# Samples 1 to 3 of a modulated linear layer by Strassen's identity, with x loaded a block earlier

## The chip, the cores and the metric

The kernel runs on one core of a Trainium2 chip. A core has TensorE (PE in the profile: matmuls, and PEld for the loading of their weights), VectorE (DVE), ScalarE (ACT), GpSimd (POOL) and SyncE (SP), which run side by side, each in its own order, and wait for each other through semaphores. DMA transfers are issued from the queues of SP, ACT and POOL and are carried by 16 DMA engines. The metric is the device time of one execution in microseconds (us). Before the change it is 1159.82 us, the median of three runs (1159.18 to 1159.86).

## What is computed

x has 4 samples of 1024 tokens with 512 features, and each sample has a condition vector. All numbers are float32. The first layer is a modulated and demodulated linear layer with a residual:

```python
ys = y * scale
d = jax.lax.rsqrt(jnp.einsum('bi,io->bo', ys * ys, weight * weight) + EPS)
out = jnp.einsum('bsi,io->bso', Efou * ys[:, None, :], weight) * d[:, None, :]
...
x = x + _L0_cond_ref(x, cond_1024, L0_cond_weight)
```

So each sample b has weights of its own (the rows of the 512x512 weight matrix scaled by ys of the sample), and each output column is scaled by d. The second layer is a mixture of experts on the result: a shared expert of width 1024 (silu(x w1) * (x w3) w2) for all tokens, and for each token two out of eight experts of width 512 (gelu between two matrices), weighted by gates; the sum divided by 3 is added to x. The change concerns the first layer alone.

## The kernel before

The 4096 tokens are cut into NB = 8 blocks of TB = 512 tokens, two for each sample (BPB = 2). KC = 4 is the number of chunks of 128 features. After the linear stage come the shared expert on blocks 0 to 5 (class Shared), the routed experts (Double, Slot), and the shared expert on blocks 6 and 7 with the gathering of the routed results. No planner orders the work: the order in which the code issues instructions is the order on each engine.

The linear stage is the loop over blk. Block 0 and the preparations (the weights' squares, the norm d, called dmod) have code of their own. For block blk it goes like this:

- load_x brings x of a block from memory in four DMAs of 256 KB, one for each group of 32 partitions, into one of the three buffers of seg3. Blocks 0 to 2 come by ACT's queue (that of block 2 is issued in norm()), the others by SP's, two blocks ahead: block blk issues the load of block blk + 2.
- turn_x (L280) transposes a chunk on VectorE, so that xT[blk] has features on partitions. There are two xT buffers, and block blk turns the x of block blk + 1.
- modulate (L268) makes the weights wm of a sample on VectorE from w0 and ys, in the block before the sample's first.
- product (L450) multiplies: for each of four output chunks oc four matmuls 128x512, one for each input chunk, into a PSUM bank of their own (pl).
- residual (L352) computes pl * dmod + xT in one VectorE instruction per chunk and writes x1T[blk], the result with features on partitions. For blocks 0 to 5 that is the tile big0 to big5, for block 6 x1T6.
- turn_back (L360) transposes the result of the block before back into rows (back), and with the last chunk store_segments issues its store to x1_d on SP (L130).
- logits_by_chunk (pq, L370) and fold_logits (pr, L386) compute the router's logits of earlier blocks on TensorE; ACT copies pq out (L379).

Between the blocks SP also loads w1 (after block 1), w3 (after block 2) and w2 (after block 4), 2 MB each, into w13 and w2_sb. VectorE makes sums of w1 and w3 for the first Shared unit (weight_sums, L431 to L434) after block 5, and sums of the tokens of block 0 (token_sums, L405 to L416) after block 6. A memset of the region called zeros, half of the tile w0t (which holds w0 before), stands on POOL after block 7; zeros is later written to memory as filling (x1s_d).

The Shared units already use Strassen's identity in Winograd's form: seven products of half size in place of eight, with sums of weights and of tokens made on VectorE. Their matmuls are 128x256 (L777, L913), and they accumulate several products in one bank, the chain, which ACT copies out between two of them.

Of the kernel before, what the change touches and what calls it, by code (L numbers as in the profile page):

```python
# [45 lines left out]
def kernel(  # L46
# [33 lines left out]
    scale = 1.0 / math.sqrt(D)  # L80
    third = 1.0 / 3.0
    early = NB - TAIL
# [15 lines left out]
    def bank_a(name):  # L98
        return ps_a.tile([P, TB], FP, tag="a", name=name)
# [12 lines left out]
    base_d = dram.tile([early * TB, D], FP, name="base_d")  # L112
    x1s_d = dram.tile([ROWS, D], FP, name="x1s_d")

    def rows_to_features(eng, tile_ap, dram_2d):

        v = dram_2d.rearrange("(g k j) o -> g j k o", g=KC, k=KC, j=Q)
        for g in range(KC):
            eng.dma_start(out=tile_ap[ts(g, Q)], in_=v[g])

    def load_segments(eng, tile_ap, dram_rows):
# [36 lines left out]
    lin = lin_ctx.enter_context(tc.tile_pool(name="lin", bufs=2))  # L158

    cond_sb = late2.tile([B, D], FP, tag="partial", name="cond_sb")  # L160
    cond_p = late2.tile([B, KC, P], FP, tag="partial", name="cond_p")
# [24 lines left out]
    def load_x(eng, blk):  # L186
        new_seg(blk)
        for g in range(KC):
            load_segments_part(eng, blk, 0, TB, g)
# [67 lines left out]
        nc.gpsimd.memset(falling[:, :, e : e + 1], float(E - e))  # L257
    steps = const.tile([P, NSLOT], FP, name="steps")
    nc.gpsimd.iota(steps, pattern=[[1, NSLOT]], base=0, channel_multiplier=0, allow_small_or_imprecise_dtypes=True)
    def by_chunk(ap):  # L260

        return ap.rearrange("p (g k j) -> p k g j", g=KC, k=KC)

    def new_wm(b):
        return lin.tile([P, KC, KC, P], FP, tag="wm", name=f"wm{b}")

    def modulate(wm, b, k):
        nc.vector.tensor_scalar(  # L268
            wm[:, k].rearrange("p k (g j) -> p k g j", g=KC),
            by_chunk(w0_sb[:, k, :]),  # L270
            ysT[:, k, b : b + 1],
            None,
            ALU.mult,
        )
# [4 lines left out]
    def turn_x(blk, k, lo=0, n=TB):  # L279
        nc.vector.transpose(xTs[blk][:, k, ds(lo, n)], segs[blk][:, ds(lo // Q, n // Q), ts(k, Q)])  # L280
# [44 lines left out]
    def norm():  # L325
        pd = bank_b("pd")
        for oc in range(KC):
            nc.tensor.matmul(
                pd[:, ds(oc * B, B)], lhsT=norm_part[:, ts(oc, P)], rhs=fold[:, :B], start=True, stop=True
            )  # L330
        pt = bank_b("pt")
        for k in range(KC):
            nc.tensor.matmul(
                pt[:, : B * E],
                lhsT=ones[:, :P],
                rhs=prod[:, k].rearrange("p b e -> p (b e)"),
                start=(k == 0),
                stop=(k == KC - 1),
            )
# [16 lines left out]
    def turn_back(blk, ks):  # L356
        if blk not in backs:
            backs[blk] = late2.tile([P, TB // Q, P], FP, tag="back", name=f"back{blk}")
        for k in ks:
            nc.vector.transpose(backs[blk][:, :, ts(k, Q)], x1T[blk][:, k, :])  # L360
        if ks[-1] == KC - 1:
            store_segments(nc.sync, x1_d[ts(blk, TB)], backs[blk])
# [3 lines left out]
    def logits_by_chunk(blk):  # L366

        pq = bank_b(f"pq{blk}")
        for k in range(KC):
            nc.tensor.matmul(  # L370
                pq[ts(k, Q)],
                lhsT=rw_pad[:, k, :],
                rhs=x1T[blk][:, k, :],
                start=True,
                stop=True,
                tile_position=(0, k * Q),
            )
        partial[blk] = late2.tile([P, TB], FP, tag="partial", name=f"partial{blk}")
        nc.scalar.activation(partial[blk], pq, AF.Copy)  # L379
# [3 lines left out]
    def fold_logits(blk, s):  # L383
        if s == 0:
            prs[blk] = bank_b(f"pr{blk}")
        nc.tensor.matmul(prs[blk][:, ds(s * E, E)], lhsT=partial[blk][:, ts(s, P)], rhs=fold, start=True, stop=True)  # L386
# [38 lines left out]
    def weight_sums(u, matrices=(0, 1)):  # L425
        for i in matrices:
# [6 lines left out]
            nc.vector.tensor_tensor(a21, a11, a21, ALU.subtract)  # L433
            nc.vector.tensor_tensor(s4, a12, s2, ALU.subtract)  # L434

    backs = {}
    for blk in range(NB):
        b = blk // BPB
        if blk < early:
            x1T[blk] = big[blk]  # L440
        elif blk == early:
            x1T[blk] = x1T6
        else:
            x1T[blk] = lin0.tile([P, KC, TB], FP, tag="w0sq", name=f"x1T{blk}")
        pas = [bank_a(f"pl{blk}_{oc}") for oc in range(KC)]
        if 2 < blk + 2 < NB:
            load_x(nc.sync, blk + 2)

        def product(oc, k, lo=0, n=TB):
            nc.tensor.matmul(  # L450
                pas[oc][:, ds(lo, n)],
                lhsT=wms[b][:, k, oc, :],
                rhs=xTs[blk][:, k, ds(lo, n)],
                start=(k == 0),
                stop=(k == KC - 1),
            )
# [18 lines left out]
        for oc in range(KC):  # L475
            if blk > 0:
                for k in range(KC):
                    product(oc, k)
                if blk > 1:
                    fold_logits(blk - 2, oc)  # L480
            if blk + 1 < NB:
                if blk > 0:
                    turn_x(blk + 1, oc)
                if (blk + 1) % BPB == 0:
                    modulate(wms[b + 1], b + 1, oc)
# [5 lines left out]
            if blk == NB - 1:  # L491
                turn_back(blk, [oc])
        if blk == 1:
            rows_to_features(nc.sync, w13[0], w1)
        if blk == 2:
            rows_to_features(nc.sync, w13[1], w3)
        if blk == 4:
            nc.sync.dma_start(out=w2_sb, in_=w2.rearrange("(k p) d -> p k d", p=P))
        if blk == early - 1:
            weight_sums(0)  # L500
        if blk == early:
            token_sums(0)
        if blk == NB - 1:
            weight_sums(1)
            nc.gpsimd.memset(zeros, 0.0)
# [239 lines left out]
    class Shared:  # L745
# [801 lines left out]
```

## Time and profile before

| | us |
|---|---|
| median of three runs | 1159.82 |
| the profiled execution's own time | 1163.28 |
| span of its trace, first to last instruction | 1161.5 |
| TensorE busy | 1145.1 (99%) |
| VectorE busy | 715.8 (62%) |
| ScalarE busy | 219.1 (19%) |
| GpSimd busy | 181.3 (16%) |
| mean granted clock of TensorE | 0.997 |

The page gives the busy time of each engine, then "the chain of work that ended last": followed back from the last instruction, at each step to what released it. The timeline shows the instructions of an engine in order of time: start, duration, engine, line, operation, what it writes and reads, the shape, how many such follow each other, and in brackets the idle time before it and what ended it. Durations of neighbouring instructions overlap a little; the step from one start to the next is what an instruction costs its engine. A float32 matmul stands as two passes in the trace, so four matmuls are "x8". The windows view gives, for each stretch, the busy time of each engine with its number of instructions, the granted clock of TensorE, the busy share of the DMA engines and the GB/s that they moved.

The linear stage takes the first 137.3 us of the span (the first matmul of a Shared unit, ch, starts there). From 27 us on TensorE is busy in it without a break.

### The profile page before, as it was taken

What the parts mean: (1) busy time and instruction counts of PE and PEld (TensorE: products, weight loads), DVE (VectorE), ACT (ScalarE), POOL (GpSimd) and SP (SyncE); (2) the same over time, 40 slices, a digit from 0 to 9 for tenths busy, and PEclk for the clock granted to TensorE, in tenths of its full rate; (3) what the DMA queues carried; (4) which work ended last, traced back from release to release, by engine and by line L of the source; (5) the groups of instructions that cost most, each with busy time, mean ns of one, the idle gap of its engine ahead of it and who ended that gap; (6) DMA issues with size and microseconds to landing.
All of it is one profiled execution on the core that took longest, in us unless ns stands there. A gap on an engine that the chain in (4) does not pass through costs nothing.

```text
span 1161.5 us, 14179 instructions
## 1 busy us (share of the span) xinstructions
PE 1145.1 (99%) x5078; PEld 947.2 (82%) x5078; DVE 715.8 (62%) x1484; ACT 219.1 (19%) x395; POOL 181.3 (16%) x220
## 2 busy tenths in 40 slices
PE   9999999999999999999999999999999998999998
PEld 6444588888888888888888888888888886888886
DVE  4547677945545455454677766677645553379987
ACT  2000032111111111111122222222222121121111
POOL 2000000012212122120000000000201100076850
PEclk9999999999999999999999999999999998999999
DMA  9599399323333247443255766657689883198971
GB/s 172 110 236 208 86 341 382 124 83 127 127 127 112 97 154 236 146 142 112 65 135 150 211 185 163 163 148 215 183 211 235 236 239 96 58 257 289 322 257 72
DMA packets 139373, 203.64 MB, mean 175 GB/s; under 512 B 9876, under 2 KB 67348, under 8 KB 139288
## 3 DMA queue, kind: packets, MB, share of 16 engines
q1 hardware_dynamic: 113080, 142.77, 43.8%
q0 software_dynamic: 14784, 47.24, 12.8%
q10 hardware_dynamic: 11424, 12.59, 3.7%
q8 instruction: 43, 0.70, 0.3%
q14 instruction: 42, 0.34, 0.1%
HBM read 120.76 MB, written 81.79 MB: 174 GB/s over the span
## 4 chain that ended last, share of the span: by engine, by line
PE 91%; DVE 3%; DMA 3%; issue 1%; ACT 1%; ACTq 0%; SPq 0%; DVEq 0%; POOLq 0%; POOL 0%
PE ch L777 18%; PE s L913 15%; PE d L1177 12%; PE pl L450 9%; PE se L777 8%; PE chd L1073 7%; PE ph L1222 6%; PE tw L777 4%; PE sed L1073 3%; PE yc L1280 3%; PE yo L1280 2%; PE twd L1073 2%; DMA seg<-in_x_dram 1%; PE pq L370 1%; PE f L939 1%
## 5 line engine op out<-in xcount | busy, mean ns | idle before, releaser
L929 DVE SCALAR_TENSOR_TENSOR base<-s,base 128x512 f32<-128x512 f32 x131 | 88.7, 687 | 77.5 <-PE s L913 77.4
L913 PE MATMUL s<-w_sb,hgh 128*128 128x256 f32 x496 | 122.7, 380 | 1.9 <-DVE base L929 1.9
L715 POOL DMA_INDIRECT x1s_d<-big,addr x64 | 64.9, 1015 | 349.7 <-DVE addr L714 328.7
L450 PE MATMUL pl<-xT,wm 128*128 128x512 f32 (+1 forms) x288 | 116.8, 554 | 0.5 <-DVE big L352 0.3
L822 ACT ACTIVATE hgh<-ch 128x512 f32<-128x512 f32 x96 | 57.3, 597 | 273.8 <-PE ch L777 266.0
L913 PEld LDWEIGHTS s<-w_sb,hgh 128*128 128x128 f32 x496 | 93.8, 190 | 16.2 <-DVE base L929 3.5
L450 PEld LDWEIGHTS pl<-xT,wm 128*128 128x128 f32 x288 | 52.5, 190 | 51.6 <-issue 47.6
L826 DVE TENSOR_TENSOR hgh<-se,hgh 128x512 f32<-128x512 f32 x64 | 44.1, 689 | 71.3 <-ACT hgh L822 62.3
L1349 POOL DMA_INDIRECT big<-ys_d,addr x64 | 71.1, 1111 | 106.8 <-DVE addr L1348 88.9
L125 POOL DMA_DIRECT2D xsegs<-x1s_d x40 | 23.3, 590 | 388.2 <-DVE big L994 296.4
L913 PE MATMUL s<-more,hgh 128*128 128x256 f32 x316 | 81.3, 380 | 0.9 <-DVE xsegs L929 0.9
L1194 DVE TENSOR_TENSOR yd<-d,yd 128x512 f32<-128x512 f32 x36 | 24.8, 689 | 71.1 <-ACT yd L1190 38.7
L913 PEld LDWEIGHTS s<-more,hgh 128*128 128x128 f32 x316 | 59.9, 190 | 9.7 <-DVE xsegs L929 1.3
L1177 PE MATMUL d<-big,hgh 128*128 128x256 f32 x288 | 66.1, 379 | 0.0
L777 PE MATMUL ch<-w0t,seg 128*128 128x256 f32 x256 | 61.0, 381 | 1.0 <-ACT hgh L822 1.0
L1177 PEld LDWEIGHTS d<-big,hgh 128*128 128x128 f32 x288 | 54.7, 190 | 7.4
L777 PE MATMUL ch<-t,seg 128*128 128x256 f32 x256 | 60.5, 379 | 0.0
L777 PEld LDWEIGHTS ch<-w0t,seg 128*128 128x128 f32 x256 | 48.2, 190 | 9.0 <-ACT hgh L822 2.6
L777 PEld LDWEIGHTS ch<-t,seg 128*128 128x128 f32 x256 | 48.6, 190 | 6.6
L777 PE MATMUL se<-big,w_sb 128*128 128x256 f32 x224 | 53.0, 379 | 0.0
L777 PE MATMUL ch<-big,w_sb 128*128 128x256 f32 x224 | 53.0, 379 | 0.0
L777 PE MATMUL tw<-big,w_sb 128*128 128x256 f32 x224 | 52.9, 379 | 0.0
(264 smaller groups left out, 1989.6 us busy)
## 6 DMA issues: line engine op xcount, KB each, us to landing
big<-in_L_cond_W1e_dram SPq DMA_DIRECT2D x88, 256.0 KB, 5.8
big<-in_L_cond_W2e_dram SPq DMA_DIRECT2D x22, 1024.0 KB, 5.5
x1s_d<-w0t SPq DMA_DIRECT2D x13, 1536.0 KB, 16.3
xsegs<-x1s_d SPq DMA_DIRECT2D x96, 128.0 KB, 3.1
ys_d<-yd SPq DMA_DIRECT2D x24, 512.0 KB, 4.4
x_d<-back SPq DMA_DIRECT2D x32, 256.0 KB, 4.6
big<-x_d SPq DMA_DIRECT2D x16, 512.0 KB, 3.7
base<-x_d SPq DMA_DIRECT2D x12, 512.0 KB, 5.2
```

Source lines behind the costliest of these rows:

```text
L450: nc.tensor.matmul(pas[oc][:, ds(lo, n)], lhsT=wms[b][:, k, oc, :], rhs=xTs[blk][:, k, ds(lo, n)], start=(k == 0), stop=(k == KC - 1),)
L715: ins = nc.gpsimd.indirect_dma_start(out=x1s_d, out_offset=bass.IndirectOffsetOnAxis(ap=at.bitcast(U32), axis=0), in_=staged(t // 2)[:, t ...
L777: nc.tensor.matmul(out, lhsT=lhs[:, k, :], rhs=rhs[:, k, :], start=start and k == 0, stop=k == KH - 1, skip_group_check=not start,)
L822: nc.scalar.activation(self.both[:, :, m, cols], self.chain, AF.Copy)
L826: nc.vector.tensor_tensor(r, bank, r, ALU.add)
L913: nc.tensor.matmul(out[:, s], lhsT=a[:, ts(s, P)], rhs=b, start=start and s == 0, stop=True, skip_group_check=not (start and s == 0),)
L929: nc.vector.scalar_tensor_tensor(r, bank, third, r, ALU.mult, ALU.add)
L1073: nc.tensor.matmul(bank[:, q], lhsT=lhs[:, k, q, :], rhs=rhs[:, k, :], start=start and q == 0 and k == 0, stop=k == KH - 1, skip_group_che ...
L1177: nc.tensor.matmul(out[:, i], lhsT=a[:, q, ts(i, P)], rhs=b[:, q, :], start=start and i == 0 and q == 0, stop=q == 1, skip_group_check=not ...
L1222: nc.tensor.matmul(self.ph[:, i], lhsT=weights[j][0][:, k, ts(c, P)], rhs=xg[j][:, k, :], start=(k == 0), stop=(k == KC - 1),)
L1280: nc.tensor.matmul(out, lhsT=a[:, k, :], rhs=b[:, k, :], start=start and k == 0, stop=k == HC // 2 - 1, skip_group_check=not start,)
L1349: nc.gpsimd.indirect_dma_start(out=picks[t][i], out_offset=None, in_=ys_d, in_offset=bass.IndirectOffsetOnAxis(ap=at.bitcast(U32), axis=0) ...
```

## The change

For samples 1 to 3 (blocks 2 to 7) the sixteen matmuls 128x512 of a block become seven products of half size, each of four matmuls 128x256. Block 0 and 1 stay as they were, apart from what they prepare for sample 1.

- modulate_whole makes wm on ACT and then adds 1/dmod ("undo") to the diagonal, with one VectorE instruction 128x128 per chunk (ident times undo plus wm). So the product times dmod holds the residual x already, and residual is not called for these blocks.
- sum_weights makes four sums of a sample's weights (128x512 each, on VectorE) in the block before the sample's first; sum_tokens makes four sums of a block's xT (two pieces of 256 tokens each) in the block before it.
- linear_by_halves issues the seven products into three banks (chain, two, other). ACT copies the chain out four times with dmod as scale (evict, two instructions 128x256 each), VectorE adds the other banks (add, six instructions 128x256 in a block), and the rest of a block's work stands between the products.
- The loads of x come a block earlier: block 1 issues those of blocks 3 and 4, block blk from 2 on that of block blk + 3. w1 is loaded by halves after blocks 2 and 3, w3 after block 4, w2 by halves after blocks 5 and 6.

The buffers of the sums are new ones (t_lin), parts of x1T6 and of zeros, and for the last sample a free weight buffer. The core of the diff:

```diff
+    nc.gpsimd.memset(ident, 0.0)
+    nc.gpsimd.affine_select(out=ident, in_=ident, ...)
...
         nc.vector.tensor_tensor(dmod, dmod, newt, ALU.mult)
+        nc.vector.reciprocal(undo, dmod)
...
+    def modulate_whole(b, k):
+        wm = wms[b]
+        nc.scalar.activation(
+            wm[:, k].rearrange("p k (g j) -> p k g j", g=KC),
+            by_chunk(w0_sb[:, k, :]), AF.Copy, scale=ysT[:, k, b : b + 1],
+        )
+        nc.vector.scalar_tensor_tensor(
+            wm[:, k, k, :], ident, undo[:, ds(k * B + b, 1)], wm[:, k, k, :], ALU.mult, ALU.add
+        )
...
+    def sum_weights(b, names):
+            1: (s1, a21, a22, ALU.add),
+            2: (s2, s1, a11, ALU.subtract),
+            7: (a21, a11, a21, ALU.subtract),
+            4: (s4, a12, s2, ALU.subtract),
...
+    def sum_tokens(blk, names):
+            3: (x_[:, K1, HI], x_[:, K2, HI], x_[:, K1, HI], ALU.subtract),
+            2: (t2, x_[:, K1, HI], x_[:, K1, LO], ALU.add),
+            1: (t1, x_[:, K2, HI], t2, ALU.subtract),
+            4: (t4, x_[:, K2, LO], t2, ALU.subtract),
...
+    def linear_by_halves(blk):
+        of = {1: (a11, x_[:, K1, LO]), 2: (a12, x_[:, K2, LO]), 3: (s4, x_[:, K2, HI]), 4: (a22, t4),
+              5: (s1, t1), 6: (s2, t2), 7: (a21, x_[:, K1, HI])}
...
+        product(chain, 1, True)
+        if more_w:
+            modulate_whole(b + 1, 0)
+            modulate_whole(b + 1, 1)
+        product(two, 2, True)
+        evict(0, LO)
+        turn_back(blk - 1, [0, 1])
+        if more_x:
+            turn_x(blk + 1, 0)
+        product(chain, 6, False)
+        add(two, 0, LO)
+        fold_logits(blk - 2, 0)
+        product(other, 7, True)
+        evict(1, LO)
+        if more_w:
+            modulate_whole(b + 1, 2)
+            modulate_whole(b + 1, 3)
+        if more_x:
+            for k in range(1, KC):
+                turn_x(blk + 1, k)
+        product(chain, 5, False)
+        evict(1, HI)
+        add(other, 1, HI)
+        logits_by_chunk(blk - 1)
+        for s in range(1, NS):
+            fold_logits(blk - 2, s)
+        turn_back(blk - 1, [2, 3])
+        if more_x:
+            sum_tokens(blk + 1, (3, 2, 1))
+        product(chain, 3, False)
+        evict(0, HI)
...
+        product(other, 4, False)
+        add(other, 1, LO)
+        if more_w:
+            sum_weights(b + 1, (1, 2))
+        if more_x:
+            sum_tokens(blk + 1, (4,))
+        if more_w:
+            sum_weights(b + 1, (7, 4))
...
-        if 2 < blk + 2 < NB:
-            load_x(nc.sync, blk + 2)
+        for n in (3, 4) if blk == 1 else (blk + 3,):
+            if 1 <= blk < NB - 3:
+                load_x(nc.sync, n)
...
+        if blk >= BPB:
+            linear_by_halves(blk)
+        for oc in range(KC) if blk < BPB else ():
...
+                turn_x(blk + 1, oc)
+                modulate_whole(b + 1, oc)
             residual(blk, oc, pas[oc])
...
+        if blk == BPB - 1:
+            sum_tokens(blk + 1, (3, 2))
+            sum_weights(b + 1, (1, 2))
+            sum_tokens(blk + 1, (1,))
+            sum_weights(b + 1, (7, 4))
+            sum_tokens(blk + 1, (4,))
-        if blk == 1:
-            rows_to_features(nc.sync, w13[0], w1)
-        if blk == 2:
+        if blk in (2, 3):
+            rows_to_features(nc.sync, w13[0], w1, (2 * blk - 4, 2 * blk - 3))
+        if blk == 4:
             rows_to_features(nc.sync, w13[1], w3)
-        if blk == 4:
-            nc.sync.dma_start(out=w2_sb, in_=w2.rearrange("(k p) d -> p k d", p=P))
+        if blk in (5, 6):
+            half = ts(blk - 5, HSC // 2)
+            nc.sync.dma_start(out=w2_sb[:, half], in_=w2.rearrange("(k p) d -> p k d", p=P)[:, half])
```

More of the change, by code (lines that the diff above doesn't have):

```diff
@@ L113, with rows_to_features @@
     x1s_d = dram.tile([ROWS, D], FP, name="x1s_d")
-    def rows_to_features(eng, tile_ap, dram_2d):
+    def rows_to_features(eng, tile_ap, dram_2d, groups=range(KC)):
         v = dram_2d.rearrange("(g k j) o -> g j k o", g=KC, k=KC, j=Q)
-        for g in range(KC):
+        for g in groups:
             eng.dma_start(out=tile_ap[ts(g, Q)], in_=v[g])
@@ L158 @@
     lin = lin_ctx.enter_context(tc.tile_pool(name="lin", bufs=2))
+    lin2 = lin_ctx.enter_context(tc.tile_pool(name="lin2", bufs=1))
+    ident = lin2.tile([P, P], FP, name="ident")
+    undo = lin2.tile([P, KC * B], FP, name="undo")
+    t_lin = lin2.tile([P, 2, TB], FP, name="t_lin")
     cond_sb = late2.tile([B, D], FP, tag="partial", name="cond_sb")
@@ L259 @@
     nc.gpsimd.iota(steps, pattern=[[1, NSLOT]], base=0, channel_multiplier=0, allow_small_or_imprecise_dtypes=True)
+    nc.gpsimd.memset(ident, 0.0)
+    nc.gpsimd.affine_select(
+        out=ident, in_=ident, compare_op=ALU.not_equal, fill=1.0, base=0, pattern=[[-1, P]], channel_multiplier=1
+    )
     def by_chunk(ap):
@@ L434, in weight_sums @@
             nc.vector.tensor_tensor(s4, a12, s2, ALU.subtract)
+    def modulate_whole(b, k):
+        wm = wms[b]
+        nc.scalar.activation(
+            wm[:, k].rearrange("p k (g j) -> p k g j", g=KC),
+            by_chunk(w0_sb[:, k, :]),
+            AF.Copy,
+            scale=ysT[:, k, b : b + 1],
+        )
+        nc.vector.scalar_tensor_tensor(
+            wm[:, k, k, :], ident, undo[:, ds(k * B + b, 1)], wm[:, k, k, :], ALU.mult, ALU.add
+        )
+    K1, K2 = slice(0, KH), slice(KH, KC)
@@ new lines, with halves_of, sums_of @@
+    spots = {}
+    def halves_of(b):
+        return [wms[b][:, ks, ds(2 * m, 2), :] for m in range(2) for ks in (K1, K2)]
+    def sums_of(b):
+        if b not in spots:
+            if b < B - 1:
+                at = [x1T6[:, n, :] for n in range(1, 4)]
+            else:
+                free = new_wm(B)
+                at = [free[:, n].rearrange("p k c -> p (k c)") for n in range(3)]
+            spots[b] = [v.rearrange("p (k q c) -> p k q c", k=KH, q=2) for v in at]
+        return spots[b]
@@ new lines, in sum_weights, with t_sums @@
+    def sum_weights(b, names):
+        a11, a12, a21, a22 = halves_of(b)
+        s1, s2, s4 = sums_of(b)
+        for n, (o, i0, i1, op) in {
+            1: (s1, a21, a22, ALU.add),
+            2: (s2, s1, a11, ALU.subtract),
+            7: (a21, a11, a21, ALU.subtract),
+            4: (s4, a12, s2, ALU.subtract),
+        }.items():
+            if n in names:
+                nc.vector.tensor_tensor(o, i0, i1, op)
+    def t_sums(blk):
+        last = x1T6[:, 0, :] if blk < early else zeros
+        return [v.rearrange("p (k t) -> p k t", k=KH) for v in (t_lin[:, 0], t_lin[:, 1], last)]
@@ new lines, in sum_tokens, with product, evict, add @@
+    def sum_tokens(blk, names):
+        x_ = xTs[blk]
+        t1, t2, t4 = t_sums(blk)
+        for n, (o, i0, i1, op) in {
+            3: (x_[:, K1, HI], x_[:, K2, HI], x_[:, K1, HI], ALU.subtract),
+            2: (t2, x_[:, K1, HI], x_[:, K1, LO], ALU.add),
+            1: (t1, x_[:, K2, HI], t2, ALU.subtract),
+            4: (t4, x_[:, K2, LO], t2, ALU.subtract),
+        }.items():
+            if n in names:
+                nc.vector.tensor_tensor(o, i0, i1, op)
+    def linear_by_halves(blk):
+        b = blk // BPB
+        x_ = xTs[blk]
+        a11, a12, a21, a22 = halves_of(b)
+        s1, s2, s4 = sums_of(b)
+        t1, t2, t4 = t_sums(blk)
+        chain, two, other = (bank_a(f"{n}l{blk}").rearrange("p (q t) -> p q t", q=2) for n in ("ch", "tw", "ot"))
+        of = {
+            1: (a11, x_[:, K1, LO]),
+            2: (a12, x_[:, K2, LO]),
+            3: (s4, x_[:, K2, HI]),
+            4: (a22, t4),
+            5: (s1, t1),
+            6: (s2, t2),
+            7: (a21, x_[:, K1, HI]),
+        }
+        def product(bank, n, start):
+            lhs, rhs = of[n]
+            for q in range(2):
+                for k in range(KH):
+                    nc.tensor.matmul(
+                        bank[:, q],
+                        lhsT=lhs[:, k, q, :],
+                        rhs=rhs[:, k, :],
+                        start=start and q == 0 and k == 0,
+                        stop=k == KH - 1,
+                        skip_group_check=not (start and q == 0),
+                    )
+        def evict(m, cols):
+            for q in range(2):
+                oc = 2 * m + q
+                nc.scalar.activation(
+                    x1T[blk][:, oc, cols], chain[:, q], AF.Copy, scale=dmod[:, ds(oc * B + b, 1)]
+                )
+        def add(bank, m, cols):
+            for q in range(2):
+                oc = 2 * m + q
+                r = x1T[blk][:, oc, cols]
+                nc.vector.scalar_tensor_tensor(r, bank[:, q], dmod[:, ds(oc * B + b, 1)], r, ALU.mult, ALU.add)
+        more_x = blk + 1 < NB
+        more_w = (blk + 1) % BPB == 0 and more_x
+        product(chain, 1, True)
[29 more added lines that the diff above has]
+        evict(0, HI)
+        if not more_x:
+            turn_back(blk, [0, 1])
+        product(other, 4, False)
[6 more added lines that the diff above has]
+            sum_weights(b + 1, (7, 4))
+        if not more_x:
+            turn_back(blk, [2, 3])
@@ L444 @@
             x1T[blk] = lin0.tile([P, KC, TB], FP, tag="w0sq", name=f"x1T{blk}")
-        pas = [bank_a(f"pl{blk}_{oc}") for oc in range(KC)]
-        if 2 < blk + 2 < NB:
-            load_x(nc.sync, blk + 2)
+        if blk < BPB:
+            pas = [bank_a(f"pl{blk}_{oc}") for oc in range(KC)]
+        for n in (3, 4) if blk == 1 else (blk + 3,):
+            if 1 <= blk < NB - 3:
+                load_x(nc.sync, n)
         def product(oc, k, lo=0, n=TB):
@@ L474 @@
             wms[b + 1] = new_wm(b + 1)
-        for oc in range(KC):
+        if blk >= BPB:
+            linear_by_halves(blk)
+        for oc in range(KC) if blk < BPB else ():
             if blk > 0:
@@ L478 @@
                     product(oc, k)
[L479 to L485, printed above, removed]
+                turn_x(blk + 1, oc)
+                modulate_whole(b + 1, oc)
             residual(blk, oc, pas[oc])
@@ L490 @@
                 turn_back(blk - 1, [oc])
-            if blk == NB - 1:
-                turn_back(blk, [oc])
-        if blk == 1:
-            rows_to_features(nc.sync, w13[0], w1)
-        if blk == 2:
+        if blk == BPB - 1:
[7 more added lines that the diff above has]
+        if blk == 4:
             rows_to_features(nc.sync, w13[1], w3)
-        if blk == 4:
-            nc.sync.dma_start(out=w2_sb, in_=w2.rearrange("(k p) d -> p k d", p=P))
+        if blk in (5, 6):
+            half = ts(blk - 5, HSC // 2)
+            nc.sync.dma_start(out=w2_sb[:, half], in_=w2.rearrange("(k p) d -> p k d", p=P)[:, half])
         if blk == early - 1:
```

## Prediction

> **What bounds the kernel now.** I read the page's engine shares first, then the chain of work in order of time through the linear stage, then the timeline of VectorE there, and last the windows around two waits. From the page:
>
> ```profile
> PE 1145.1 (99%) x5078; PEld 947.2 (82%) x5078; DVE 715.8 (62%) x1484; ACT 219.1 (19%) x395; POOL 181.3 (16%) x220
> ...
> PE 91%; DVE 3%; DMA 3%; issue 1%; ACT 1%; ACTq 0%; SPq 0%; DVEq 0%; POOLq 0%; POOL 0%
> ```
>
> TensorE is the bound: 99% busy and 91% of the chain. The chain in order of time, one block of the linear stage, and two later pieces:
>
> ```profile
> 77.19 0.99 PE pq L370 x8
> 78.19 3.63 PE pl L450 x8
> ...
> 81.94 3.54 PE pl L450 x8
> ...
> 92.91 0.99 PE pq L370 x8
> ...
> 136.28 1.01 PE pr L386 x10
> ...
> 207.74 1.73 PE ch L777 x8
> ```
>
> A block takes 92.91 - 77.19 = 15.72 us with no wait in it: four groups of products (four matmuls 128x512, eight passes in the trace), one pq, four pr. A group of four 128x256 matmuls, as the Shared units already issue them, takes 1.73. A pr pass costs about 0.10 (1.01 for ten), half of it shown in the group behind it when they stand singly.
>
> VectorE in block 1, and in block 6 the sums that this change multiplies:
>
> ```profile
> 32.76 0.71 DVE L280 STREAM_TRANSPOSE xT<-seg 128x512 f32<-128x512 f32 x1 [3.84 <-DMA seg<-in_x_dram]
> 33.40 0.45 DVE L268 TENSOR_SCALAR wm<-w0t,ysT 128x512 f32<-128x512 f32 x1
> 33.76 0.75 DVE L352 SCALAR_TENSOR_TENSOR big<-pl,dmod,xT 128x512 f32<-128x512 f32 x1
> 34.42 0.70 DVE L360 STREAM_TRANSPOSE back<-big 128x512 f32<-128x512 f32 x1
> 35.05 0.67 DVE L280 STREAM_TRANSPOSE xT<-seg 128x512 f32<-128x512 f32 x1
> ...
> 122.71 0.65 DVE L405 TENSOR_TENSOR big<-big 128x512 f32<-128x512 f32 x1
> 123.39 0.69 DVE L416 TENSOR_TENSOR w0t<-big 128x512 f32<-128x512 f32 x1
> 124.11 1.29 DVE L413 TENSOR_TENSOR w0t<-big,w0t 128x512 f32<-128x512 f32 x2
> ```
>
> From start to start: a turn of x 0.64, a modulation 0.36, a residual 0.66, a turn back 0.63, a sum 0.62, or 0.70 where the next needs it. Block 1 can't begin on VectorE before x of block 2 has landed at 32.7, while TensorE has matmuls of block 1 until 42.24 (where the last residual of block 1 starts). The windows over the loads, and over the one long wait of TensorE:
>
> ```profile
> 24.00:28.00 4.00, 3.71 (x16) 2.57 (x15) 2.86 (x9) 0.94 (x2) 0.00 (x0) 1.00 1.23 182
> ...
> 966.00:970.00 4.00, 0.00 (x0) 0.00 (x0) 0.64 (x2) 0.00 (x0) 0.00 (x0) 1.00 0.82 246
> 970.00:974.00 4.00, 3.16 (x8) 2.54 (x9) 2.11 (x5) 0.00 (x0) 0.00 (x0) 0.50 0.46 168
> 974.00:978.00 4.00, 4.00 (x14) 3.25 (x13) 1.10 (x4) 0.38 (x1) 0.00 (x0) 0.64 0.00 0
> ```
>
> The last three columns are granted clock, DMA share and GB/s: while x is loaded all 16 DMA engines are busy (1.23); and after a wait of 5.3 us (ph on W2e) the clock ran at 0.50 and 0.64 for two windows, (1 - 0.50) x 4 + (1 - 0.64) x 4 = 3.4 us lost.
>
> **The change part by part.**
>
> *Products.* Blocks 2 to 7: 16 matmuls 128x512 become 28 of 128x256, seven groups of 1.73 = 12.1; pq 0.99 stays; one pr alone is 0.22, three together 0.6 + 0.1. Sum 14.0 for 15.72, so 1.69 a block, **-10.1** over six. All of it is on the path, since TensorE waits for nothing there now.
>
> *Undo.* One RECIPROCAL 128x16 more, in the row of tiny operations before block 0's residuals, which TensorE waits for (pl on big, 0.3). The existing one steps 0.29: **+0.3**. The identity's two operations lie on POOL, idle after 12 us; needed at 39.
>
> *Loads of x.* Block 1 now queues x of blocks 3 and 4 on SP. Block 4's part waits only for VectorE's turns of block 1, done at 23.3, so SP issues it from 23.3 to 25.2. ACT issues block 2's x from 23.5, and its last two quarters now wait for block 3's quarters, since the built order deals the completion semaphores out over both queues in turn; the last goes out behind all of block 4's. 1.05 MB at 182 to 189 GB/s (windows 16 to 28) is 5.7 us, so x of block 2 lands at 32.7 + 5.7 = 38.4. A turn needs all four quarters. Behind it on VectorE stand block 1's four rounds (turn 0.64, diagonal 0.2, residual 0.66, turn back 0.63: 2.1 each) and then the sums; behind those the store of block 0 and the load of block 5 on SP, which have 20 us to spare. The rounds end at 46.8; then t3, t2, s1, s2 in that order (0.70 + 0.62 + 0.70 + 0.70): s2 is ready at 49.5. TensorE reaches the product that needs s2 and t2 at 42.24 + 0.3 + 2 x 1.73 = 46.0. So **+3.5** of new waiting, 0.7 of it inside the second product, whose last quarter of xT is turned only at 45.4, and 2.8 in one piece. Bounds: if block 2's x isn't delayed, the rounds end with the last residual's matmul, 42.5 + 1.3, and s2 at 46.5: 0.5. At the 128 GB/s of the window 28 to 32 it lands at 40.9: 6.0. I take 3.5, because the rate next to it is 182.
>
> *VectorE's work.* Before: four turns, residuals, turns back: 7.7 a block, modulations apart. After: turns and turns back 5.1, six adds of 128x256 from PSUM, four sums (2.7), a score (0.1). An add has no row of its own in this stage; 128x256 sums of L431 to L434 step 0.34, and the full residual 0.66 is the other end; I take 0.36, so 10.1 a block. The diagonal add 128x128 lies between 0.1 (a score, 128x32) and 0.36 (L268): 0.2. Blocks 3 and 5 add four of these and four weight sums, 13.6; block 5 also the w1/w3 sums that stand there now (8 x 0.36), 16.5; block 6 the token sums, 12.8. Against 14.0 of TensorE only blocks 5 and 6 together are over (29.3 to 28.0), and VectorE enters them ahead: block 4 leaves it 3.9. The end of block 6 may wait a little: **+0.3**, bounds 0 and, if an add costs 0.66, about 4. VectorE's waits for x (25.7 in the list of waits) go, but cost nothing today.
>
> *ACT.* The modulations of samples 1 to 3, 0.36 each on VectorE, become 0.63 each on ACT (row of L287), and eight evictions of 128x256 a block (0.38 each, row of L856) come to it. That is at most 6.2 of its 14 us (8 x 0.38 + 4 x 0.63 + 0.6); today it is busy 0.6 per block. The chain bank is read while another product of 1.73 runs, two evictions need 0.8: hidden, with 0.9 to spare.
>
> *Weights.* w1 by halves in blocks 2 and 3, w3 in block 4, w2 by halves in 5 and 6. The tightest is w3: with blocks of 14.0, block 4 runs from 74 to 88, block 3's store goes out 11 us into it and w3 behind it; 3.1 MB at 210 GB/s (window 50 to 63: 207) from 86 on is there by 101. VectorE's sums want it when block 5's own work is done, about 105. Hidden, 4 us to spare. w2 comes by 125, wanted near 150. The memset of zeros moves behind block 7's last product (about 130); the fills that read it went out at 149.9 and now at about 144. No price.
>
> **Sum.** -10.1 + 0.3 + 3.5 + 0.3 = -6.0. The stages behind the linear one are timed from its end and shift as they are. The profiled execution took 1163.28 (span 1161.5 and 1.8 around it), 3.5 above the median 1159.82, as much as the half clock cost there; I don't know whether the unprofiled runs had that stretch. The profiled one would come to 1157.3, the median to **1153.8**.
>
> **Rivals.** 0.2% is 2.3 us, about what a measurement of this kernel can tell from no change.
>
> (A) Block 2's x isn't late, because its queue is served first: 3.5 becomes 0.5, 1150.8. For it: two of its quarters go out before block 4's last two. Against: a turn needs all four, and x of block 3, issued by SP from 16.3, landed in quarters at 22.2 to 26.4, 1.4 apart, with block 1's x of ACT's queue through at 20.7: the queues look served in order of issue.
>
> (B) The wait in block 2 drops the clock: +3.4 (the price from the windows above), 1157.2, and 1159.7 with the wait at 6.0. For it the 5.3 us wait that did; against it that the longest piece is 2.8. [...]
>
> (C) VectorE sets the pace in blocks 3, 5 and 6, adds from PSUM costing near 0.66: +3 more, 1156.8.
>
> (D) Slower: VectorE sets the pace in all six blocks. Its work there is 10.1, 13.6, 10.1, 16.5, 12.8 and some 7 = 70 of TensorE's 84. To lose, it must pass 84 + 6.0 + 2.3 = 92, that is, run 31% above the rows I used; at 40% above it is 98, some 14 over 84, and the time 1168. The sums read two pieces of 256, but L405 does so too at 0.65.
>
> (E) The stretch at half clock near 970 falls away because the wait before it shifts: 1150.4. It is against this that the wait itself stays 5.3.
>
> **How the numbers follow.** Forecast 0.56 (1151.3 to 1156, from the wait's bounds), A 0.13, B 0.13, C 0.08, D 0.05, E 0.05. The range 1150.0 to 1158.0 leaves out D, the upper half of B and the far ends. Faster by over 0.2% (below 1157.5): forecast, A, E, most of C and over half of B: 0.86. Within 0.2%: the rest of B and C: 0.07. Slower: D and a wait longer than its bound: 0.07.
>
> **What would show it.** Groups of the new products at 1.73 and later blocks of 14.0; VectorE's first turn of block 2's x at about 38.4; a wait of TensorE on VectorE near 46 to 49.5, in two pieces; no wait above 1 us in blocks 3 to 7; ch of the first Shared unit at 131 instead of 137.3; clock 1.00 from 45 to 60. Wrong would be: PE waits in every block (C, D), a clock of 0.5 near 50 (B), or a first turn at 33 (A).

## The result, and the profile after

The changed kernel takes 1155.51 us (median of 6 runs, 1154.53 to 1157.23), the kernel before, on the same chip, 1159.59 (median of 6, 1157.79 to 1160.52). The ratio is 0.9967 with a 95% interval of 0.9954 to 0.998, so the change gains 4.1 us, between 2.3 and 5.3. The prediction was 1153.8 in a range of 1150.0 to 1158.0.

The profiled execution took 1156.11 (span 1154.3). From the page of the changed kernel, the engine shares:

```profile
PE 1135.5 (98%) x5222; PEld 974.4 (84%) x5222; DVE 735.1 (64%) x1533; ACT 246.5 (21%) x455; POOL 181.8 (16%) x222
```

TensorE has 9.6 us less work (1145.1 before), in 144 passes more, since a pass of 128x256 takes half as long as one of 128x512 (eight step 1.73, where they stepped 3.54). VectorE and ScalarE have taken over 19 and 27 us. TensorE is still the bound, at 98%.

The timeline of TensorE in the changed kernel shows block 2, block 6 with the first groups of block 7, and the first product of a Shared unit:

```profile
42.10 1.89 PE L527 MATMUL chl<-xT,wm 128*128 128x256 f32 x8
43.83 0.59 PE L527 MATMUL twl<-xT,wm 128*128 128x256 f32 x2
45.36 1.53 PE L527 MATMUL twl<-xT,wm 128*128 128x256 f32 x6 [0.93 <-DVE xT L289]
49.49 1.97 PE L527 MATMUL chl<-t_lin,x1T 128*128 128x256 f32 x8 [2.60 <-DVE x1T L488]
51.30 0.28 PE L396 MATMUL pr<-fold,partial 128*128 128x8 f32 x2
...
102.81 1.89 PE L527 MATMUL chl<-xT,wm 128*128 128x256 f32 x8
104.54 1.89 PE L527 MATMUL twl<-xT,wm 128*128 128x256 f32 x8
106.26 1.89 PE L527 MATMUL chl<-t_lin,wm 128*128 128x256 f32 x8
107.99 0.28 PE L396 MATMUL pr<-fold,partial 128*128 128x8 f32 x2
108.13 1.97 PE L527 MATMUL otl<-xT,wm 128*128 128x256 f32 x8
109.94 1.89 PE L527 MATMUL chl<-t_lin,wm 128*128 128x256 f32 x8
111.76 1.06 PE L380 MATMUL pq<-big,rw_pad 128*32 128x512 f32 x8
112.76 0.84 PE L396 MATMUL pr<-fold,partial 128*128 128x8 f32 x6
113.45 1.98 PE L527 MATMUL chl<-xT,wm 128*128 128x256 f32 x8
115.26 1.89 PE L527 MATMUL otl<-w0t,wm 128*128 128x256 f32 x8
116.98 1.89 PE L527 MATMUL chl<-xT,wm 128*128 128x256 f32 x8
...
131.97 1.98 PE L940 MATMUL ch<-big,w_sb 128*128 128x256 f32 x8
```

Read the starts, not the durations. A block without a wait takes 116.98 - 102.81 = 14.17, where it was 15.72. Of its seven groups four step 1.72 to 1.73; the three with a pr before them or a pq behind them step 1.81 or 1.82. Block 2 has the two brackets that the prediction asked for, 0.93 and 2.60, both on VectorE. They stretch the way from the block's first matmul to the first pr from 5.18 (experiment e6, below, has it without a wait) to 9.20, so the two waits of 3.53 cost 4.0. The brackets say less because a group's duration, 1.89, runs 0.16 past its step of 1.73, so that each bracket begins late, and because the group behind a wait takes a little longer (1.97).

The first ch of a Shared unit starts at 131.97, where the timeline of before has 137.15: 5.2 earlier. From the list of TensorE's waits over the span of the changed kernel (total, number, longest), the longest one and those of the linear stage:

```profile
PE ph L1385 <- issue: 3.9, 1, 3.9
PE chl L527 <- DVE x1T L488: 2.6, 1, 2.6
...
PE twl L527 <- DVE xT L289: 0.9, 1, 0.9
...
PE pl L611 <- DVE xT L289: 0.6, 1, 0.6
...
PE pl L611 <- DVE big L362: 0.3, 1, 0.3
```

The two entries pl end by 27.07, chl and twl are the two in block 2; the timeline has no bracket in blocks 3 to 7. The long one, ph, stands near 960, in the expert stage; it was 5.3 before. The two spans differ by 7.2, not 5.2, because this wait is shorter and a little less of the stretch at half clock behind it falls on matmuls. The profiled execution of before also took 1163.28, against a median of 1159.59. The medians, not this pair of executions, say what the change is worth.

VectorE in block 1 of the changed kernel, in order of time:

```profile
38.18 0.71 DVE L289 STREAM_TRANSPOSE xT<-seg 128x512 f32<-128x512 f32 x1 [9.18 <-DMA seg<-in_x_dram]
...
48.66 0.69 DVE L488 TENSOR_TENSOR x1T<-x1T,wm 128x512 f32<-128x512 f32 x1
```

VectorE sits idle for 9.18 us until x of block 2 has landed, begins its rounds at 38.18 where it began at 32.76, and has s2 ready at 49.35. TensorE goes on at 49.49. In the windows of the same kernel all DMA engines are busy until 36, 4 us longer than before (the window 28 to 32 had 0.85 and 128 GB/s, the next one 0.01):

```profile
28.00:32.00 4.00, 4.00 (x16) 1.41 (x15) 0.99 (x2) 0.09 (x1) 0.00 (x0) 1.00 1.24 183
32.00:36.00 4.00, 4.00 (x10) 1.71 (x9) 0.00 (x0) 2.34 (x4) 0.00 (x0) 1.00 1.24 182
```

### The profile page after: what moved, and what is told of

Read it like the earlier page. It is cut to its first block, busy times and chain, and to the rows that moved or that the text cites. A ratio compares the mean times of both kernels' runs of the same rounds, so it can differ in the third digit from the quotient of the medians.

```text
span 1154.3 us, 14608 instructions
## 1 busy us (share of the span) xinstructions
PE 1135.5 (98%) x5222; PEld 974.4 (84%) x5222; DVE 735.1 (64%) x1533; ACT 246.5 (21%) x455; POOL 181.8 (16%) x222
## 5 line engine op out<-in xcount | busy, mean ns | idle before, releaser
L940 PE MATMUL ch<-big,seg 128*128 128x256 f32 x224 | 52.9, 379 | 0.0
L940 PEld LDWEIGHTS se<-big,w_sb 128*128 128x128 f32 x224 | 42.6, 190 | 6.5 <-issue 0.8
```

Source lines behind the costliest of these rows:

```text
L940: nc.tensor.matmul(out, lhsT=lhs[:, k, :], rhs=rhs[:, k, :], start=start and k == 0, stop=k == KH - 1, skip_group_check=not start,)
```

## The experiments

The theory was: the change saves TensorE 1.5 us in each of six blocks, and gives 4.0 of these 9.3 back once, in block 2, because x of block 4 now travels ahead of x of block 2. The rivals were that VectorE's own work is the limit, that the new order of loads has a price of its own, and that the wait moves the clock. The ratios below are against the kernel before on the same chip; "ch" is the start of the first Shared unit's first product, 137.15 before and 131.97 after. e5 and e7 were run once each, so they are read by their traces and not by their time.

| kernel | us (runs) | ratio, 95% | ch |
|---|---|---|---|
| after, again | 1155.72 (12) | 0.9965, 0.9953 to 0.9978 | 133.38 |
| e1: x of block 4 later | 1151.65 (5) | 0.9942, 0.9928 to 0.9956 | 129.18 |
| e2: weights' sums first | 1151.96 (5) | 0.9941, 0.9927 to 0.9954 | 129.76 |
| e3: new loads alone | 1161.84 (10) | 1.0020, 1.0007 to 1.0032 | 139.11 |
| e4: products with the old loads | 1159.38 (10) | 0.9998, 0.9989 to 1.0007 | 136.87 |
| e5: wait lengthened | 1163.01 (1) | | 139.16 |
| e6: e1 and e2 together | 1150.28 (6) | 0.9920, 0.9903 to 0.9937 | 128.03 |
| e7: more sums on VectorE | 1159.09 (1) | | 136.63 |

**e1: x of block 4 goes out behind block 1's store.**

```diff
-        for n in (3, 4) if blk == 1 else (blk + 3,):
-            if 1 <= blk < NB - 3:
-                load_x(nc.sync, n)
+        if 1 <= blk < NB - 3:
+            load_x(nc.sync, 3 if blk == 1 else blk + 3)
...
+        if blk == 1:
+            load_x(nc.sync, 4)
```

> The changed kernel with one edit: x of block 4 is loaded after block 1's store instead of at block 1's start. Theory 1 (block 2's x is late because block 4's x shares the queues with it): the first turn of block 2's x comes back from 38.2 to about 32.7; s2 is ready at 42.1 + 1.3 + 2.7 = 46.1 and TensorE asks for it at 42.1 + 2 x 1.73 = 45.6, so the wait in block 2 falls from 3.5 to about 0.5; the first Shared product starts near 129.0 instead of 132.0, the time is 3 us below the changed kernel's. Theory 2 (VectorE simply has too much to do before block 2: four rounds and eight sums): the wait stays near 3 us wherever block 4's x is loaded, and the time is the changed kernel's.

Measured, from the timelines of VectorE and TensorE of e1:

```profile
32.09 0.71 DVE L289 STREAM_TRANSPOSE xT<-seg 128x512 f32<-128x512 f32 x1 [2.84 <-DMA seg<-in_x_dram]
...
44.09 1.89 PE L527 MATMUL twl<-xT,wm 128*128 128x256 f32 x8
46.70 1.97 PE L527 MATMUL chl<-t_lin,x1T 128*128 128x256 f32 x8 [0.73 <-DVE x1T L488]
```

With one transfer moved, the first turn is back at 32.09, the second product runs in one piece and the wait is 0.73. ch comes 2.8 earlier, and the median is 7.5 below before on its chip, where the changed kernel's is 4.1 below on its own. So the late x is the cause of most of the wait, and x is late because of block 4's transfer, as theory 1 said. The 0.73 that is left is VectorE's own work behind block 1's last residual; e6 takes it away.

**e2: sample 1's weights and their sums before the turns of block 2's x**, the loads as in the changed kernel.

```diff
+                if oc == 0:
+                    for k in range(KC):
+                        modulate_whole(b + 1, k)
+                    sum_weights(b + 1, (1, 2, 7, 4))
                 turn_x(blk + 1, oc)
-                modulate_whole(b + 1, oc)
...
-            sum_tokens(blk + 1, (3, 2))
-            sum_weights(b + 1, (1, 2))
-            sum_tokens(blk + 1, (1,))
-            sum_weights(b + 1, (7, 4))
-            sum_tokens(blk + 1, (4,))
+            sum_tokens(blk + 1, (3, 2, 1, 4))
```

> The changed kernel with block 4's load left where it is, but sample 1's weights are made at once on ScalarE and their diagonal and four sums done on VectorE before the turns of block 2's x, in the 9.2 us in which VectorE waits for it. Theory 1: x still lands at 38.2, but behind it stand only four rounds of 1.9 and two sums: t2 is ready at 38.2 + 7.6 + 1.4 = 47.2 instead of 49.4, and the wait in block 2 falls from 3.5 to about 1.6; time 1.9 below the changed kernel's, Shared near 130.1. Theory 2 (VectorE's work): the same gain would come, but with this edit and the later load together only the larger of the two. If ScalarE's modulations in a row delay the logits' copy, a new wait on pq appears: then less.

From the timeline of TensorE of e2:

```profile
44.17 2.10 PE L527 MATMUL twl<-xT,wm 128*128 128x256 f32 x8
47.29 1.96 PE L527 MATMUL chl<-t_lin,x1T 128*128 128x256 f32 x8 [1.02 <-DVE t_lin L504]
```

The waits in block 2 shrink to 1.0 for t2 and 0.2 inside the second product (2.10 for 1.89), and ch is at 129.76, close to the 130.1 expected. The median gained more than the expected 1.9: it is 7.2 below before on its chip, 3.1 more than the changed kernel's 4.1. This fills the idle time of VectorE in place of removing it; it is worth as much as e1 within the intervals. The order of VectorE's work is thus a second handle on the same wait, not another cause.

**e3: the new order of loads in the kernel before**, with no product changed.

```diff
-        if 2 < blk + 2 < NB:
-            load_x(nc.sync, blk + 2)
+        for n in (3, 4) if blk == 1 else (blk + 3,):
+            if 1 <= blk < NB - 3:
+                load_x(nc.sync, n)
```

(The loads of w1, w3 and w2 are moved as in the change, too.)

> The kernel before with the new order of loads alone (x a block earlier, w1, w3, w2 spread), the linear stage as it was. Theory 1: block 2's x lands at 38.2 here too; the last chunk is turned at 38.2 + 3 x 2.26 + 0.7 = 45.7, while TensorE asks for it at 42.2 + 3 x 0.88 = 44.9: a wait of about 1 us once, then VectorE's waits for x in blocks 2 to 6 are gone and give nothing, since TensorE doesn't wait for them. Time 0.5 to 1.5 above the kernel before. Rival: the loads by themselves are worth something (DMA traffic spread): faster than before by 1 us or more.

```profile
44.23 1.13 PE L451 MATMUL pl<-xT,wm 128*128 128x512 f32 x2 [0.26 <-DVE wm L268]
46.47 1.13 PE L451 MATMUL pl<-xT,wm 128*128 128x512 f32 x2 [1.11 <-DVE wm L268]
```

The same late x (VectorE waits 9.6 for it) makes TensorE wait in the kernel before, too, there for the weights of sample 1. The price is over what was expected (0.5 to 1.5): ch is 2.0 later, and the median 2.7 above before (the interval of the ratio is 0.8 to 3.7 us). This is the part of the change that loses.

**e4: the changed products with the old order of loads.**

```diff
-        for n in (3, 4) if blk == 1 else (blk + 3,):
-            if 1 <= blk < NB - 3:
-                load_x(nc.sync, n)
+        if 2 < blk + 2 < NB:
+            load_x(nc.sync, blk + 2)
...
-        if blk in (2, 3):
-            rows_to_features(nc.sync, w13[0], w1, (2 * blk - 4, 2 * blk - 3))
+        if blk == 1:
+            rows_to_features(nc.sync, w13[0], w1)
+        if blk == 2:
+            rows_to_features(nc.sync, w13[1], w3)
         if blk == 4:
-            rows_to_features(nc.sync, w13[1], w3)
...
+            nc.sync.dma_start(out=w2_sb, in_=w2.rearrange("(k p) d -> p k d", p=P))
```

> The changed kernel with the old order of loads (x two blocks ahead, w1 after block 1, w3 after block 2, w2 after block 4). Theory 1: the wait in block 2 falls to 0.5 as with the later load, but x of block 5 now stands behind w3 and lands near 83 to 84, when VectorE wants to turn it at about 75; the adds of block 4 stand behind the turn, and TensorE waits 3 to 6 us in block 4. Shared starts between 131.5 and 135, the time is 0 to 3 us above the changed kernel's. Rival: loads a block earlier are not needed, since the old ones were hidden for TensorE: then the time is 3 us below the changed kernel's.

Timeline of TensorE, and the windows of the same run:

```profile
71.92 1.99 PE L527 MATMUL otl<-x1T,wm 128*128 128x256 f32 x8 [1.08 <-DVE big L547]
...
90.02 2.58 PE L527 MATMUL otl<-x1T,wm 128*128 128x256 f32 x8 [3.33 <-DVE big L547]
```

```profile
88.00:92.00 4.00, 1.98 (x8) 1.68 (x9) 3.97 (x10) 0.78 (x2) 0.00 (x0) 0.91 1.22 200
92.00:96.00 4.00, 4.00 (x14) 3.31 (x13) 3.97 (x9) 0.53 (x2) 0.00 (x0) 0.66 1.00 226
```

With the old loads x arrives too late in blocks 3 and 4: VectorE waits 5.7 us for x of block 4 and 5.6 for x of block 5 (whose load stands behind the 2 MB of w3 in SP's order, and whose first turn starts at 85.93), and its add holds up TensorE, 1.08 in block 3 and 3.33 in block 4. Behind the wait of 3.33 the clock is down (0.91 and 0.66 in the last-but-two column). Nothing is left of the gain. That is more than was expected, which had only block 4's wait and ch between 131.5 and 135; it came at 136.87, and block 2 had begun 1.0 late here (43.09 for 42.10). So earlier loads are needed for x of blocks 4 and 5; only as early as in front of block 2's x is too early.

**e5: the wait in block 2 made longer.** Eight sums whose result is overwritten are added before block 1's sums.

```diff
         if blk == BPB - 1:
+            for _ in range(8):
+                nc.vector.tensor_tensor(t_lin[:, 0, :], xTs[blk + 1][:, 0, :], xTs[blk + 1][:, 1, :], ALU.add)
```

> After block 1's last residual VectorE makes eight sums 128x512 more (into t_lin, which the real sums overwrite; they are work added for the test), so everything behind them, the sums that TensorE waits for among it, comes 8 x 0.62 = 5.0 later. It prices rival (B). [...] Rival (a wait in the linear stage doesn't touch the clock, since the stretch near 962 has another cause): clock 1.00 throughout, ch at 137.0, the time 5.0 over the kernel after, about 1160.5.

TensorE's timeline and the windows of e5, cut every 3.41 us from the steps of the clock's record, a fall at 51.50 and a rise at 58.33:

```profile
55.11 3.55 PE L527 MATMUL chl<-t_lin,x1T 128*128 128x256 f32 x8 [8.41 <-DVE x1T L488]
58.49 0.28 PE L396 MATMUL pr<-fold,partial 128*128 128x8 f32 x2
```

```profile
44.67:48.09 3.42, 1.53 (x6) 1.06 (x6) 3.35 (x7) 0.32 (x1) 0.00 (x0) 1.00 0.18 41
48.09:51.50 3.41, 0.00 (x0) 0.00 (x0) 3.24 (x6) 0.00 (x0) 0.00 (x0) 1.00 0.96 217
51.50:54.91 3.41, 0.00 (x0) 0.00 (x0) 3.31 (x6) 0.00 (x0) 0.00 (x0) 0.50 0.95 214
54.91:58.33 3.42, 3.22 (x8) 2.62 (x9) 3.42 (x7) 0.00 (x0) 0.00 (x0) 0.50 0.89 143
```

The clock falls to 0.50 for 6.83 us, two windows, the group behind the wait steps 3.38 in place of 1.8, and ch is 7.2 later than in the changed kernel. Of this 5.6 is the later start of the group behind the wait (55.11 for 49.49) and 1.6 the half clock behind it (84.05 from there to ch, for 82.48). So a wait in the linear stage does move the clock, and the rival of a wait that leaves the clock alone is out. The price was known before only as 3.4, from the stretch near 970.

**After, again: the same kernel beside e5 to e7.**

> The changed kernel once more, beside e6 on the same chip. 1155.5 within 1.2 of it either way; ch of the first Shared unit at 132.0 and TensorE's two waits in block 2 at 0.9 and 2.6 again, since nothing in them depends on chance; the clock in block 2 at 1.00 if the idle time is split over two of the clock's windows of 3.4 us again, at 0.50 for one of them if it isn't. The stretch at half clock near 962 is 3.4 or 6.8 long, by where its wait falls.

In this run of the unchanged code ch is at 133.38. The waits in block 2 are 0.66 and 2.61, where they were 0.93 and 2.60, but behind them the clock was halved:

```profile
49.23 2.47 PE L527 MATMUL chl<-t_lin,x1T 128*128 128x256 f32 x8 [2.61 <-DVE x1T L488]
...
51.78 3.05 PE L527 MATMUL otl<-xT,wm 128*128 128x256 f32 x8
```

Windows cut every 3.41 us from a step of the clock's record, of this run (a fall at 50.55) and then of the first profile of the changed kernel (counted back from the fall at 962.52, 267 x 3.413 behind 51.15):

```profile
43.73:47.14 3.41, 2.23 (x10) 1.33 (x8) 3.38 (x7) 0.84 (x2) 0.00 (x0) 1.00 0.00 0
47.14:50.55 3.41, 1.32 (x6) 1.22 (x7) 3.38 (x6) 0.00 (x0) 0.00 (x0) 1.00 0.88 198
50.55:53.96 3.41, 3.41 (x10) 2.81 (x10) 3.41 (x7) 0.84 (x2) 0.00 (x0) 0.50 0.90 218
```

```profile
44.32:47.74 3.42, 1.64 (x7) 1.06 (x6) 3.39 (x7) 0.55 (x2) 0.00 (x0) 1.00 0.03 7
47.74:51.15 3.41, 1.66 (x8) 1.51 (x9) 3.38 (x7) 0.00 (x0) 0.00 (x0) 1.00 0.95 214
51.15:54.56 3.41, 3.41 (x19) 3.03 (x18) 3.41 (x8) 0.84 (x2) 0.00 (x0) 1.00 0.97 226
```

The second column is TensorE's busy time. In the first table the idle time (by the profile's record of TensorE) falls into the windows as 1.18 and 2.09, and the next window runs at 0.50; in the second it is split 1.78 and 1.75, and the clock holds. So the same kernel pays 1.7 in one execution (84.15 from the group behind the wait to ch, for 82.48) and nothing in another. The waits of the two are the same within 0.27; what differs is where in them the windows begin. ch is only 1.4 later because the first wait was 0.27 shorter. e7, below, has block 2's waits at 0.78 and 2.61, split as 1.49 and 1.89 (counted back from its stretch at 0.50 near 969), and its clock held. Seven of the 18 runs of the changed kernel have a mean granted clock of 0.995 or 0.996, none of the 38 of before under 0.997; that fits, but only the profiled ones show the place. As an estimate from these means over the whole span, before loses 2.0 us to half clock on average and the changed kernel 3.3. The 1.3 between them is about what separates the 5.2 of a profile with the clock up in block 2 from the 3.9 between the means of these runs (1159.55 and 1155.66).

**e6: e1 and e2 together, and the reciprocal behind block 0's residuals** (the diffs of both, and:)

```diff
-        nc.vector.reciprocal(undo, dmod)
...
+        if blk == 0:
+            nc.vector.reciprocal(undo, dmod)
```

> Block 4's x behind block 1's store (as in e1), sample 1's weights and their sums made ahead of the turns of block 2's x (as in e2), and the reciprocal for undo behind block 0's residuals. Theory 1 (the transfer of block 4's x ahead of block 2's makes block 2's x late, and that is the whole of the wait): no wait above 0.2 for a VectorE sum is left in block 2, the reciprocal gives back 0.25 to 0.3, ch at 129.2 - 0.7 - 0.3 = 128.2 to 128.5, and the time 0.7 to 1.0 below e1, about 1150.8, -4.7 against the kernel after. Rival (the first product of block 2 is held by VectorE's own work behind block 1's last residual, so that the order of loads and sums doesn't matter any more): ch stays at 129.0 to 129.2 as in e1, the time at 1151.6.

```profile
42.18 1.89 PE L526 MATMUL chl<-xT,wm 128*128 128x256 f32 x8
43.91 1.89 PE L526 MATMUL twl<-xT,wm 128*128 128x256 f32 x8
45.63 1.89 PE L526 MATMUL chl<-t_lin,x1T 128*128 128x256 f32 x8
47.36 0.28 PE L395 MATMUL pr<-fold,partial 128*128 128x8 f32 x2
```

No bracket is left: block 2 runs like the others, ch is at 128.03, and the time is 0.9920 of before (0.9903 to 0.9937), 9.6 us by the medians and 5.4 below the changed kernel on the same chip. That is better than both kernels and about what the products alone save. Moving the reciprocal can't be told from chance: block 2 begins 0.18 earlier than in e1, where 0.25 to 0.3 was expected, and that start lies anywhere from 42.02 to 42.45 in the other six profiles with these products, e4's apart. The rival, a floor at e1's ch, is out.

**e7: four sums more on VectorE in each of blocks 2 to 6**, their result overwritten.

```diff
         if more_x:
+            for _ in range(4):
+                nc.vector.tensor_tensor(t_lin[:, 1, :], xTs[blk + 1][:, 0, :], xTs[blk + 1][:, 1, :], ALU.add)
             sum_tokens(blk + 1, (3, 2, 1))
```

> Four sums 128x512 more on VectorE in each of blocks 2 to 6, 4 x 0.65 = 2.6 a block and 13 in all, into a buffer that the real sums overwrite; work added for the test. VectorE is busy for 14.0, 11.2, 12.6, 11.2 and 13.9 in the five blocks of the kernel after, 63.0 of 71.0. Theory (VectorE is not the bound, but near it; rivals C and D are wrong by a margin of some 8): no wait of TensorE before block 4 or 5, and 13 - 8 = 5, from 3 to 7, of waits by the end of block 6; ch at 135 to 139, the time 3 to 7 over the kernel after, without what the clock may add. Rival (C: VectorE already sets the pace in blocks 3, 5 and 6, its work only hidden by what TensorE does anyway): waits of 2 or more in block 3 and in each block behind it, 8 to 13 in all, ch at 140 to 145.

Timeline of TensorE in e7, the brackets behind block 2:

```profile
79.46 1.97 PE L527 MATMUL chl<-t_lin,x1T 128*128 128x256 f32 x8 [1.61 <-DVE x1T L488]
...
109.66 1.97 PE L527 MATMUL chl<-t_lin,wm 128*128 128x256 f32 x8 [1.61 <-DVE wm L488]
...
119.43 1.99 PE L527 MATMUL otl<-w0t,wm 128*128 128x256 f32 x8 [0.54 <-DVE x1T L547]
```

Of 13 us of added work TensorE feels 4.7 (ch at 136.63), 3.9 of it in waits from block 4 on, as expected; block 3 has none. VectorE had about 8 us to spare over these blocks, as its busy time in the changed kernel says (14.0, 11.2, 12.6, 11.2 and 13.9 of 71.0). It is close behind TensorE, but not the bound.

## Why the prediction was right, and where not

The prediction held in its mechanism: the products gained on the path of TensorE, and x of block 2 came late by the time worked out. The sum said -6.0 for the linear stage, and the stage gives -5.2 in one profile and -3.8 in the other; the medians give -4.1. Its terms:

- Products, -10.1: measured 6 x 1.55 = -9.3, in ch terms (blocks 3 to 6 from 15.72 to 14.17; block 2 and the last block within 0.1 of that). The mechanism was right, the term 0.8 too large. All seven groups were taken at 1.73, 12.1 in sum; they measure 12.34, since three of them step 0.09 more beside a pr or a pq. Two of these the prediction had, inside its prices of pr: the lone pr comes to 0.14 and 0.09 behind it, for 0.22. It left out the one ahead of the pq, and the three pr take 0.69 by themselves, where it had 0.6.
- Undo, +0.3: the reciprocal is there at 26.07, but it covers the copy behind it. The residuals start 0.12 later against dmod, and TensorE's wait for them goes from 0.29 to 0.33. Almost nothing, and less than that wait differs between executions (0.21 in the second profile of the changed kernel).
- The wait in block 2, +3.5: 0.93 + 2.60 by the list of waits, landing at 38.1 for 38.4, s2 at 49.35 for 49.5. This was the best step of the working. It took the wait as the whole price: by the starts it costs 4.0. e1 shows the cause. The last two quarters of x of block 2 were issued at 24.84 and 26.30, each just after a quarter of block 3's x had landed (24.82 and 26.28), as the working said.
- The end of block 6, +0.3: no wait. The adds step 0.37 to 0.40 and the diagonal add 0.23, close to the 0.36 and 0.2 that were taken; e7 shows the room. VectorE's busy time in blocks 3 to 6 is 49.0, where the working had 53.0.
- ACT, weights, store: no wait in blocks 3 to 7, so hidden, as said. VectorE's new waits for ACT's modulations (4.7 in four pieces) touch nothing.

9.3 less 4.0 and 0.1 (block 2 begins at 42.10 for 42.04) is the 5.2 of the first profile. The products were taken 0.8 too large and the wait 0.5 too small; that the sum missed this by 0.8 and not 1.3 is luck, since the two small terms of 0.3 came to nothing. What the sum had no term for is the clock, which was a rival:

- (A), block 2's x not late: out, the first turn is at 38.18. e1 is what it would have been.
- (B), the clock drops in block 2: it was held unlikely because the longest piece is 2.8 and the stretch in the profile of before followed 5.3; what a wait of 2.8 does, no trace of before showed. This was the step that failed. After pieces of 0.66 and 2.61 the clock did halve, in one of two profiles. Its price was too high: 3.4 was the loss of two windows at half clock (6.8 us near 970), and one window costs 1.7 at most, (1 - 0.50) x 3.41, which it did here. The profile with it gains 3.8 (its wait being 0.27 shorter), the one without it 5.2, and the median of 4.1 lies between.
- (C) and (D), VectorE sets the pace: out, since no wait stands in blocks 3 to 7; e7 shows the margin.
- (E), the stretch near 970 falls away: it didn't go in any of the ten profiles at hand, but it is one window long in some and two in others. It did go in some runs that were not profiled: one of the 18 of the changed kernel and 4 of the 38 of before have a mean clock of 1.0 over the span, which leaves less than 0.6 us for half clock. They took 1154.76, and 1157.71 to 1158.29.

Left open: the wait of ph near 960 is 5.3 and 4.6 in the two profiles with the old products and 2.8 to 3.9 in the eight with the new ones. No run here shows why, and the medians, which follow ch within 0.8 in all of e1 to e4 and e6, show no gain of its size. The two profiled executions with 5.3 and 4.6 took 1163.28 and 1163.58, against medians of 1159.59 and 1161.84, so these waits may not be the usual ones of those kernels.

## What to carry to other kernels

When transfers are issued earlier, work out in which order the queues serve them all: the one moved forward can land in front of the one that is needed next, and one load put back behind it was worth about 3 us here, where the whole change had brought 4. After cutting work on the bounding engine, look at its first block, where the new preparations have had the least time, and fill the other engine's idle time there with work that needs no new data. Count short waits on TensorE that lie close together with the chance of a halved clock behind them: the two in block 2, of 0.66 and 2.61, were followed by 0.50 in one profile of the changed kernel, and of 0.93 and 2.60 by 1.00 in the other.

## What the runs showed of the hardware

- The granted clock. In the ten profiles every stretch at 0.50 between the first 10 us and the last one of the span is 3.41 or 6.83 us long. In before it runs from 970.03 to 976.86 and the next fall is 184.32 later, 54 x 3.413; in the changed kernel it runs from 962.52 to 969.34, with the same 184.32 behind it. The windows of 3.41 above are cut on this raster, also where the record has no step. The stretch begins 0.81 before the end of ph's wait in before, 1.78 before it in the changed kernel's first profile, and 1.32 behind the end of block 2's second wait in the changed kernel's second profile. Ahead of each stretch is a window in which TensorE was idle for about 2.1 us or more (2.09 in that second profile is the least), and windows with 1.78 (the changed kernel), 1.88 (e5) and 1.89 (e7) idle, while the clock was up, were followed by 1.00. What 1.9 to 2.09 does, no profile shows. As an estimate from these windows, a wait of 2.8 us can cost up to 1.7 more, (1 - 0.50) x 3.41, or nothing, by where it falls. Once it was down, the clock came back after a window with about 0.54 (e2) idle or less, and stayed down for a second window where the first had 0.81 (before), 1.17 (e5, near 970), 1.78 (the changed kernel, near 963), 2.51 (e3) or 3.41 (e5, block 2) idle.
- The transfers. x of block 4 (issued by SP from 23.3 to 25.2) and x of block 2 (by ACT from 23.5) shared the DMA engines at 182 to 184 GB/s, and their quarters landed in turn: block 2's at 30.4, 33.7, 36.5 and 38.1, three of block 4's at 31.7, 35.5 and 37.9 (the landing of its first is not told). Neither queue was served first; apart from one pair (36.5 and 37.9) these seven landed in the order of their issue.
- Each of TensorE's two waits in block 2 cost about 0.25 more than its bracket says: 3.53 in sum by the brackets, 4.02 by the starts. The bracket begins where the last record ends, 0.16 past its step; the rest is the slower first group (1.97 for 1.89).
